# Dense products of a transformer layer written as four column tiles each, with the scheduler's table of draws removed

## The chip, the cores and the metric

The kernel runs on one core of a Trainium2 chip. The metric is the device time of one execution in microseconds (us). The kernel before took a median of 1049.04 us over three runs (1048.99 to 1049.08).

## What is computed

One macaron layer in fp32 on x of shape (4, 1024, 256): a feed-forward half step, causal attention with 16 heads of 16 features, a second feed-forward half step with the same weights.

```python
x = x + 0.5 * ffn(layernorm(x))
x = x + attn(layernorm(x), Wq, Wk, Wv, Wo)
x = x + 0.5 * ffn(layernorm(x))

def ffn(x):                      # 256 -> 704 -> 256
    g = (x @ gate_w.T) * gate_s
    u = (x @ up_w.T) * up_s
    return ((silu(g) * u) @ down_w.T) * down_s

def attn(x):                     # 16 heads of 16
    q, k, v = x @ Wq.T, x @ Wk.T, x @ Wv.T       # rotary embedding on q and k
    p = softmax(q @ k.T / 4 + causal_mask)
    return (p @ v) @ Wo.T
```

## The kernel before, in words

**Blocks.** The 4096 tokens are cut into 8 blocks of 512 (`BLK`); two blocks make one sequence of the batch. Each block goes through `ffn(i, 1)`, `qkv(i)`, the attention of four groups of four heads (`max_half`, `row_of_max`, `exp_half`, `weigh`, `attended`), `project` and `ffn(i, 2)`.

**Three shapes of product.** TensorE works in three shapes, and the planner names them `full`, `row` and `col`.

- `full`: the stationary operand is 128 rows by 128 columns. These are the dense products: gate and up (line 582, 512 wide), down (line 649, 256 wide), the features of q and k (line 723, 512 wide), the values (line 762, 256 wide) and the output projection (line 1104, 256 wide). The transposes at the start and in block 0 (lines 478 and 523) and the transpose that turns the row of maxima (line 943) have this shape too.
- `row`: a head has 16 features, and lies on 16 or 17 of 32 partitions. Four such products stand one above the other in the array. These are the scores for the maxima (line 863, q stationary) and the scores again for the exponentials (line 978, k stationary, one more row carries the negative maximum).
- `col`: the weighted values (line 1025). The stationary operand is 128 keys by 32 columns of one head, and four heads stand side by side, each with moving data of its own and each with 32 of the 128 output partitions.

An fp32 product is one instruction in the program, and the trace shows it as two loads of weights (LDWEIGHTS) and two passes (MATMUL). A transpose is one load and one pass.

**Order.** Every instruction is written out by a planner in Python (`Planner`, line 51). It keeps a clock for each engine with estimated durations, and at each step places the operation that can start first. Score halves are placed in pairs, called bursts: usually one half for maxima and one for exponentials. Up to `VISIT = 2` bursts follow one another before PE goes back to other work; below, such a stretch of one or two bursts is a visit. `GAP` is the least PE time between visits, `LONG` the PE time up to which a visit is put off until its second burst can follow, `WAIT` and `CHANGE` are what a change of shape is given, `HOLD` and `PATIENCE` delay a `col` product while PE is in shape `full`. `DRAWS` (line 23) is a table of 36 seeds, one for every 8 bursts (`draw`, line 155): a seed varies these constants and adds random numbers to the priorities.

**The row of maxima.** DVE writes each head's negative maxima to a column of `nm` (line 915, place by `row_at`, line 847). When a group is complete, PE transposes 128 columns of `nm` (line 943) so that the group's 16 columns land on 16 partitions of a bank, ACT copies them to `nmT` (line 948), and SP sends them by DMA to the free row of `qT` (line 953).

Of the kernel before, what the change touches and what calls it, by code (L numbers as in the profile page):

```python
# [19 lines left out]
P = 128  # L20
EPS = 1e-5
MASKED = -1e30
DRAWS = (
    490404, 660007, 210038, -148846, 520673, 329115, 0, 984430, -467682, -480220, 442636, -673967, -166110,
    -50883, 108124, 486735, -702287, -116672, -983856, -198212, 600534, -536043, -117586, -276618, -971831,
    -28682, -76214, -968411, -277199, -633759, -338722, 457662, -446958, -796892, -654951, -323475,
)


class Buf:  # L30
# [6 lines left out]
class Op:  # L37

    def __init__(self, eng, us, emit, deps=(), takes=(), uses=(), prio=5, tail=0.2, mode="full"):
        self.eng, self.us, self.emit, self.tail, self.mode = eng, us, emit, tail, mode
        self.takes, self.uses, self.prio = list(takes), list(uses), prio
        self.deps = [d for d in deps if d is not None]
        self.then = []
        self.done, self.waiters, self.pending, self.order = None, [], None, None
        for b in self.takes + self.uses:
            b.left += 1


class Planner:
# [1 line left out]


    ENGINES = ("pe", "dve", "act", "pool", "dma")
    GAP = 2.0
    LONG = 8.0
    VISIT = 2
    SECOND = 0.3
    OPEN = 3.0  # L60
    DUE = 0.5
    WAIT = dict(full=0.1, row=0.1, col=0.3)
    CHANGE = dict(full=0.2, row=0.2, col=0.12)
    HOLD = 0.8
    PATIENCE = 4.0

    STRETCH = 8

    def __init__(self, kinds, shared, draws=()):
        self.draws, self.bursts, self.luck, self.random = draws, 0, dict.fromkeys(self.ENGINES, 0.0), None  # L70
        self.draw()
        self.shared = shared
        self.busy = dict.fromkeys(self.ENGINES, 0.0)
        self.free = {k: [(0.0, i) for i in range(n)] for k, n in kinds.items()}
        self.loose = {e: [] for e in self.ENGINES}
        self.queues = {e: {} for e in self.ENGINES}
        self.mode, self.since, self.visit = "full", 9.0, 0
        self.alloc = None
        self.log = []
        self.added, self.unplaced = 0, 0  # L80
# [74 lines left out]
    def draw(self):  # L155

        if self.bursts % self.STRETCH:
            return
        n = self.bursts // self.STRETCH
        seed = self.draws[n] if n < len(self.draws) else 0  # L160
        for k in ("GAP", "LONG", "SECOND", "DUE", "HOLD", "PATIENCE", "OPEN"):
            setattr(self, k, getattr(Planner, k))
        self.luck = dict.fromkeys(self.ENGINES, 0.0)
        if seed:
            r = self.random = Random(abs(seed)).random
        if seed < 0:
            for k in ("GAP", "LONG", "SECOND", "DUE", "HOLD", "PATIENCE", "OPEN"):
                setattr(self, k, getattr(Planner, k) * (0.97 + 0.06 * r()))
        elif seed:
            self.GAP, self.LONG, self.SECOND = 0.8 + 1.8 * r(), 4.0 + 5.0 * r(), 0.05 + 0.5 * r()  # L170
            self.DUE, self.HOLD, self.PATIENCE, self.OPEN = r(), 1.6 * r(), 2.0 + 4.0 * r(), 1.0 + 3.0 * r()
            self.luck = {e: max(0.0, 4.0 * r() - 2.0) for e in self.ENGINES}

    def step(self, burst):
# [5 lines left out]
        for eng in self.ENGINES:  # L180
            for c in self.candidates(eng):
                s = max(c[0], self.busy["pe"] + 0.05) if eng == "pe" else c[0]
                if c[2].mode == "col" and self.mode == "full" and self.busy["pe"] < self.ready(c[2]) + self.PATIENCE:
                    s += self.HOLD
                if eng == "pe" and due and any(k.slot is None and k.kind == "d" for k in c[2].takes):
                    s += self.DUE
                key = (s, c[1] + (self.luck[eng] * self.random() if self.luck[eng] else 0.0))
                if best is None or key < best[0]:
                    best = (key, c)
# [59 lines left out]
def tile_macaron(  # L249
# [59 lines left out]
    for kind, (n, _) in shapes.items():  # L309
# [13 lines left out]
    lasting = dict(  # L323
        kT=[cpool.tile([P, NG, BLK], F32, name=f"kT_{i}", tag=f"kT_{i}") for i in range(3)],
        hL=[cpool.tile([P, BLK], F32, name=f"hL_{i}", tag=f"hL_{i}") for i in range(1)],
        nm=[cpool.tile([P, P + 32], F32, name=f"nm_{i}", tag=f"nm_{i}") for i in range(3)],
        va=[cpool.tile([P, NB, H * VS + HP - VS], F32, name=f"va_{i}", tag=f"va_{i}") for i in range(4)],
    )

# [90 lines left out]
    def norm(i, j, src, prio, kind):  # L420
# [51 lines left out]
        ]  # L472
        return a, [*b, *v, c, d, *e], list(zip(xns, e))

    def idle(d, n):

        for _ in range(n):
            nc.tensor.matmul(d.tile[:, :P], ident, ident, start=True, stop=True)
# [36 lines left out]
    def turned(pair, j, xnT, prio, later, view, idles=0):  # L515

        ds = [Buf("d") for _ in range(NC)]

        def emit():
            idle(ds[0], idles)  # L520
            for c, d in enumerate(ds):
                for n, (xn, _) in enumerate(pair):
                    nc.tensor.transpose(d.tile[:, ts(n, P)], xn.tile[:, ts(c, P)], ident)  # L523

        def copy(c):
            (nc.vector.tensor_copy if c else nc.scalar.copy)(
                view(xnT.tile[:, c])[:, j - 1 : j + 1],
                ds[c].tile[:, : 2 * P].rearrange("p (j a t) -> p j a t", j=2, t=HP),
            )

        t = Op("pe", 4 * 0.107, emit, [p[1] for p in pair], [*ds, xnT], [p[0] for p in pair], prio=prio)
        k = [Op("act", act_us(D), partial(copy, 0), [t], uses=[ds[0], xnT], prio=later)]
        return t, [*k, Op("dve", dve_us(D), partial(copy, 1), [t], uses=[ds[1], xnT], prio=later)]


    def ffn(i, which):
# [38 lines left out]
        def product(d, cols, takes, parts=1):  # L575

            n = NB // parts
            for part in range(parts):
                for k in range(NC):

                    def emit(k=k, j=part * n):
                        nc.tensor.matmul(  # L582
                            d.tile[:, j * P : (j + n) * P],
                            wgu_sb[:, k, cols],
                            view(xnT.tile[:, k])[:, j : j + n],
                            start=(k == 0),
                            stop=(k == NC - 1),
                        )

                    need = [*(copies[part * NC : part * NC + NC] if parts > 1 else copies), gu_loaded]  # L590
                    first = not part and not k
                    o = Op(
                        "pe", mm_us(BLK // parts), emit, need, takes if first else [], [xnT] if first else [d, xnT], prio=3
                    )
                    mids.append(o)
            return o
# [43 lines left out]
        for j in range(NB):  # L640

            def down(j=j):
# [3 lines left out]

                def emit(n):
                    c = chunks[n]
                    nc.tensor.matmul(  # L649
                        d.tile[:, :D], hT[c].tile[:, ts(j, P)], wd_sb[:, c, :], start=(n == 0), stop=(n == NI - 1)  # L650
                    )

# [43 lines left out]
    def qkv(blk):  # L696
# [21 lines left out]
        def features(g):  # L718
# [1 line left out]
            d, qc, qs = Buf("d"), Buf("qc"), Buf("qs")  # L720

            def product(k):
                nc.tensor.matmul(  # L723
                    d.tile, wqkv_sb[:, k, ts(g, P)], xnT.tile[:, k, :], start=(k == 0), stop=(k == NC - 1)
                )

# [31 lines left out]
        def values(j):  # L758
            d = Buf("d")

            def product(n, k):
                nc.tensor.matmul(  # L762
                    d.tile[:, ts(n, D)],
                    xnT.tile[:, k, ts(j + n, P)],
                    wqkv_sb[:, k, 2 * D :],
                    start=(k == 0),
                    stop=(k == NC - 1),
                )
# [77 lines left out]

    def row_at(g, part, h, j):


        return g % 2 * P + part * GH * NB + h * NB + j  # L850

    def max_half(blk, unit, pair, nm, reduces):

# [24 lines left out]
        def head(e):  # L878
# [14 lines left out]
            if unit[0][0] != unit[-1][0]:  # L893
                j, part = unit[0][1:3]

                def reduce():
                    o = row_at(0, part, 2 * pair + e, j)
                    nc.vector.tensor_reduce(
                        nm.tile[:, o : o + P + 1 : P],
                        sc[e].tile.rearrange("p (g k) -> p g k", g=2),  # L900
                        AX.X,
                        ALU.max,
# [25 lines left out]
    def row_of_max(blk, g, nm, reduces):  # L928
# [11 lines left out]
            loose_att.extend(need)  # L940

        def turn():
            nc.tensor.transpose(d.tile[:, :P], nm.tile[:, g % 2 * HP : g % 2 * HP + P], ident)  # L943

        def copy():

            r = g % 2 * (P - HP)
            nc.scalar.copy(t.tile, d.tile[r : r + GH * NB, :P])

        def send(pair):  # L950
            for h in (2 * pair, 2 * pair + 1):
# [3 lines left out]
                    in_=t.tile[a : a + NB, :],  # L955
                )

        p = Op("pe", 0.107, turn, need, [d, t], [nm], prio=1)
        c = Op("act", act_us(P), copy, [p], uses=[d, t], prio=1)
        loose_att.append(c)  # L960
        for pair in (1, 0):
# [137 lines left out]
    def project(blk, j, aTs):  # L1099
        e = Buf("d")  # L1100

        def product():
            for c in range(NC):
                nc.tensor.matmul(  # L1104
                    e.tile[:, :D], aTs[c].tile[:, ts(j, P)], wo_sb[:, c, :], start=(c == 0), stop=(c == NC - 1)
                )

# [203 lines left out]
```

## Time and profile before

| | |
|---|---|
| median of 3 runs | 1049.04 us |
| the profiled execution | 1049.1 us |
| its span, first to last instruction | 1047.4 us |
| TensorE: busy, passes | 1041.7 us (99%), 6550 |
| granted TensorE clock | 1.000 of full speed |
| VectorE (DVE), ScalarE (ACT), GpSimd (POOL) busy | 809.2, 431.4, 295.2 us |
| packets of PE's instruction queue | 51 of 16 KB |

Busy time of PE counts a pass from its start to its modelled end, and passes overlap: a pass of 512 columns is listed with some 600 ns, while the next one starts 429 ns after it. So the mean duration of a PE group says less than the distance between two starts, and the working below goes by starts.

### The profile page before, as it was taken

The numbers are of one execution on the slowest core, as the hardware profiler recorded it, in microseconds if no ns is written. First come the engines' busy times: TensorE is split into PE (matmuls) and PEld (weight loads), VectorE is DVE, ScalarE is ACT, GpSimd is POOL, SyncE is SP. The second block draws the span as 40 slices with busy tenths as digits, with TensorE's granted clock in tenths as the row PEclk, the third lists the DMA queues.
The fourth block names the chain that finished last, engine by engine and source line by source line (L and its number), as shares of the span: only waits on it lengthen the run. The fifth ranks groups of instructions, "written<-read, shape, count | busy, mean of one in ns | idle before, by whom it ended". The sixth has DMA issues, their size and how long they took to land.

```text
span 1047.4 us, 17496 instructions
## 1 busy us (share of the span) xinstructions
PE 1041.7 (99%) x6550; PEld 535.2 (51%) x6550; DVE 809.2 (77%) x1876; ACT 431.4 (41%) x821; POOL 295.2 (28%) x501
## 2 busy tenths in 40 slices
PE   9999999999999999999999999999999999999998
PEld 5655554454545644553544554543645544535365
DVE  6679879788898887778888797698898876884342
ACT  3215333344454353444434443355354443453511
POOL 5322521431131622412204524221216211121210
PEclk9999999999999999999999999999999999999999
DMA  8211202101010110111111012001021010010000
GB/s 289 60 41 42 48 15 61 41 22 41 21 42 22 41 42 21 37 46 37 38 29 31 12 42 41 31 13 41 2 62 42 11 51 2 21 42 11 11 21 20
DMA packets 37924, 40.38 MB, mean 39 GB/s; under 512 B 3984, under 2 KB 27728, under 8 KB 37712
## 3 DMA queue, kind: packets, MB, share of 16 engines
q1 hardware_dynamic: 37184, 38.81, 13.5%
q8 instruction: 51, 0.84, 0.3%
q10 hardware_dynamic: 656, 0.47, 0.2%
q14 instruction: 33, 0.27, 0.1%
HBM read 19.60 MB, written 15.20 MB: 33 GB/s over the span
## 4 chain that ended last, share of the span: by engine, by line
PE 98%; DVE 1%; DMA 0%; ACT 0%; issue 0%; SPq 0%; DVEq 0%
PE bank L582 29%; PE bank L863 17%; PE bank L649 17%; PE bank L1025 13%; PE bank L978 10%; PE bank L723 5%; PE bank L1104 3%; PE bank L762 3%; PE bank L943 0%; DMA x<-in_x 0%; PE bank L523 0%; DVE nm L915 0%; DVE bank L888 0%; ACT pT L987 0%; DVE st L425 0%
## 5 line engine op out<-in xcount | busy, mean ns | idle before, releaser
L987 ACT ACTIVATE pT<-bank 128x512 f32<-128x512 f32 x576 | 299.4, 601 | 316.3 <-PE bank L978 315.3
L915 DVE TENSOR_REDUCE nm<-bank 128x1 f32<-128x512 f32 (+2 forms) x640 | 331.0, 573 | 25.8 <-PE bank L978 25.3
L582 PE MATMUL bank<-xnT,wgu_sb 128*128 128x512 f32 (+1 forms) x708 | 320.9, 598 | 0.2 <-ACT pT L987 0.2
L863 PE MATMUL bank<-kT,qT 16*128 16x512 f32 (+3 forms) x1536 | 291.1, 509 | 0.5 <-DVE hT L629 0.5
L978 PE MATMUL bank<-qT,kT 17*128 17x512 f32 (+3 forms) x1536 | 291.4, 513 | 0.0
L999 POOL TENSOR_SCALAR_AFFINE_SELECT pT<-pT 128x256 f32<-128x256 f32 x256 | 99.4, 407 | 406.4 <-ACT pT L987 405.7
L582 PEld LDWEIGHTS bank<-xnT,wgu_sb 128*128 128x128 f32 x708 | 127.8, 190 | 163.3 <-issue 121.3
L863 PEld LDWEIGHTS bank<-kT,qT 16*128 16x128 f32 x1536 | 112.9, 184 | 134.1 <-issue 38.2
L649 PE MATMUL bank<-wd_sb,hT 128*128 128x256 f32 x640 | 150.0, 380 | 0.0
L1025 PE MATMUL bank<-pT,va 128*32 128x512 f32 (+3 forms) x1536 | 137.1, 490 | 0.0
L649 PEld LDWEIGHTS bank<-wd_sb,hT 128*128 128x128 f32 x640 | 121.0, 190 | 19.1 <-issue 2.9
L888 DVE TENSOR_TENSOR bank<-bank,causal 128x256 f32<-128x256 f32 (+1 forms) x320 | 103.8, 370 | 25.9 <-PE bank L978 22.1
L978 PEld LDWEIGHTS bank<-qT,kT 17*128 17x128 f32 x1536 | 111.7, 184 | 8.3 <-issue 4.0
L623 ACT ACTIVATE ta<-bank,gus_sb 128x512 f32<-128x512 f32 x80 | 55.0, 688 | 115.0 <-PE bank L582 110.3
L626 DVE SCALAR_TENSOR_TENSOR ta<-ta,bank 128x512 f32<-128x512 f32 x80 | 54.8, 685 | 51.5 <-ACT ta L623 50.6
L1025 PEld LDWEIGHTS bank<-pT,va 128*32 128x32 f32 x1536 | 44.1, 109 | 94.0 <-issue 65.4
L629 DVE SCALAR_TENSOR_TENSOR hT<-bank,gus_sb,ta 128x512 f32<-128x512 f32 x80 | 59.4, 743 | 17.6 <-PE bank L582 16.9
L655 DVE TENSOR_TENSOR x<-bank,x 128x256 f32<-128x256 f32 x64 | 26.7, 418 | 56.1 <-PE bank L649 56.0
L1064 POOL TENSOR_TENSOR oq<-oq 128x512 f32<-128x512 f32 x32 | 40.6, 1268 | 102.0 <-DVE oq L1061 95.6
L1061 DVE STREAM_TRANSPOSE oq<-bank 128x512 f32<-128x512 f32 x64 | 45.4, 709 | 22.3 <-PE bank L1025 22.0
L723 PE MATMUL bank<-xnT,wqkv_sb 128*128 128x512 f32 x128 | 60.2, 603 | 0.0
L734 POOL TENSOR_TENSOR qs<-qs,rope_sb 128x512 f32<-128x512 f32 x32 | 40.6, 1271 | 40.3 <-DVE qs L731 40.0
(61 smaller groups left out, 670.6 us busy)
## 6 DMA issues: line engine op xcount, KB each, us to landing
xd<-xs SPq DMA_DIRECT2D x84, 128.0 KB
xnT<-xd SPq DMA_DIRECT2D x21, 512.0 KB
kT<-qT SPq DMA_DIRECT2D x64, 64.0 KB
x<-in_x SPq DMA_DIRECT2D x7, 512.0 KB
out<-x SPq DMA_DIRECT2D x14, 256.0 KB
qT<-nmT SPq DMA_DIRECT2D x128, 2.0 KB
wgu_sb<-in_wgu SPq DMA_DIRECT2D x2, 512.0 KB
rope_sb<-in_rope SPq DMA_DIRECT2D x1, 1024.0 KB
```

The source lines that it names most:

```text
L582: nc.tensor.matmul(d.tile[:, j * P : (j + n) * P], wgu_sb[:, k, cols], view(xnT.tile[:, k])[:, j : j + n], start=(k == 0), stop=(k == NC - 1),
L623: nc.scalar.activation(a.tile, d.tile, AF.Tanh, scale=gus_sb[:, 0, c : c + 1])
L629: nc.vector.scalar_tensor_tensor(hT[c].tile, e.tile, gus_sb[:, 1, c : c + 1], a.tile, ALU.mult, ALU.mult)
L649: nc.tensor.matmul(d.tile[:, :D], hT[c].tile[:, ts(j, P)], wd_sb[:, c, :], start=(n == 0), stop=(n == NI - 1))
L723: nc.tensor.matmul(d.tile, wqkv_sb[:, k, ts(g, P)], xnT.tile[:, k, :], start=(k == 0), stop=(k == NC - 1))
L863: nc.tensor.matmul(sc[e].tile[:, c0 : c0 + w], qT[blk].tile[r, g, ts(j, P)], kt.tile[r, g, :w], start=True, stop=True,)
L888: nc.vector.tensor_tensor(d, d, causal.unsqueeze(1).to_broadcast([P, len(masked), P]), ALU.add)
L915: nc.vector.tensor_reduce(nm.tile[:, o : o + 1], sc[e].tile[:, c0 : c0 + w], AX.X, ALU.max, negate=True)
L978: nc.tensor.matmul(sc[e].tile[:, c0 : c0 + w], kt.tile[r, g, ts(k % NB, P)], qT[blk].tile[r, g, BLK - w :], start=True, stop=True,)
L987: nc.scalar.activation(pT.tile[:, e, :w], sc[e].tile[:, :w], AF.Exp)
L999: nc.gpsimd.affine_select(out=d, in_=d, compare_op=ALU.is_ge, fill=0.0, base=0, pattern=[[0, 2], [1, P]], channel_multiplier=-1,)
L1025: nc.tensor.matmul(av.tile[ts(r, HP), BLK - w :], va[base + k // NB].tile[:, k % NB, h * VS : h * VS + HP], pTs[u, r // 2].tile[:, r % 2, ...
```

## The change

Each dense product is written as four products with 32 stationary columns each, on four column tiles, with the same moving operand and 32 output partitions each. This is the shape of the weighted values, so only two shapes are left, `row` and `col`, but for the transposes of the start and of block 0. The row of maxima is turned by an ordinary product with the identity on one column tile (32 columns of `nm`), and `nm` shrinks from 160 to 64 columns. The table of draws is empty, `HOLD` and `PATIENCE` go, and `GAP`, `LONG` and one `WAIT` have other values.

```diff
-DRAWS = ( 490404, 660007, 210038, -148846, ... 36 seeds ... )
+DRAWS = ()
...
-    GAP = 2.0
-    LONG = 8.0
+    GAP = 0.8
+    LONG = 7.0
...
-    WAIT = dict(full=0.1, row=0.1, col=0.3)
+    WAIT = dict(full=0.1, row=0.1, col=0.1)
     CHANGE = dict(full=0.2, row=0.2, col=0.12)
-    HOLD = 0.8
-    PATIENCE = 4.0
...
-                if c[2].mode == "col" and self.mode == "full" and self.busy["pe"] < self.ready(c[2]) + self.PATIENCE:
-                    s += self.HOLD
...
-        nm=[cpool.tile([P, P + 32], F32, name=f"nm_{i}", tag=f"nm_{i}") for i in range(3)],
+        nm=[cpool.tile([P, 2 * HP], F32, name=f"nm_{i}", tag=f"nm_{i}") for i in range(3)],
...
+    def product_of(out, w, x, **kw):
+
+        for m in range(w.shape[1] // HP):
+            nc.tensor.matmul(out[ts(m, HP)], w[:, ts(m, HP)], x, **kw)
...
# gate and up; the same edit for down, q and k, values and the output projection
-                        nc.tensor.matmul(
+                        product_of(
                             d.tile[:, j * P : (j + n) * P],
                             wgu_sb[:, k, cols],
                             view(xnT.tile[:, k])[:, j : j + n],
...
-        return g % 2 * P + part * GH * NB + h * NB + j
+        return g % 2 * HP + part * GH * NB + h * NB + j
...
-            nc.tensor.transpose(d.tile[:, :P], nm.tile[:, g % 2 * HP : g % 2 * HP + P], ident)
+            nc.tensor.matmul(d.tile[:HP, :P], nm.tile[:, ts(g % 2, HP)], ident, start=True, stop=True)
...
-            r = g % 2 * (P - HP)
-            nc.scalar.copy(t.tile, d.tile[r : r + GH * NB, :P])
+            nc.scalar.copy(t.tile, d.tile[: GH * NB, :P])
```

Operations have the mode `col` unless they say otherwise; the transposes of `turned` say `full`. The planner begins in `col`.

## The prediction

> **What bounds the kernel.** I read the page's busy times first, then its chain, then the groups of PE by shape, then PE's waits, and last the timeline at two places.
>
> ```profile
> span 1047.4 us, 17496 instructions
> ...
> PE 1041.7 (99%) x6550; PEld 535.2 (51%) x6550; DVE 809.2 (77%) x1876; ACT 431.4 (41%) x821; POOL 295.2 (28%) x501
> ...
> PE 98%; DVE 1%; DMA 0%; ACT 0%; issue 0%; SPq 0%; DVEq 0%
> PE bank L582 29%; PE bank L863 17%; PE bank L649 17%; PE bank L1025 13%; PE bank L978 10%; PE bank L723 5%; PE bank L1104 3%; PE bank L762 3%; PE bank L943 0%; DMA x<-in_x 0%; PE bank L523 0%; DVE nm L915 0%; DVE bank L888 0%; ACT pT L987 0%; DVE st L425 0%
> ```
>
> TensorE is the bound: the chain is PE from end to end. The next view, waits that ended an idle time of PE, says that it hardly ever waits: 2.4 us in all, 1.7 of them before the first dense product.
>
> ```profile
> PE bank L478 <- POOL ident masks.py:199: 1.4, 1, 1.4
> PE bank L863 <- DVE hT L629: 0.5, 1, 0.5
> PE bank L523 <- ACT xn L451: 0.3, 1, 0.3
> PE bank L582 <- ACT pT L987: 0.2, 1, 0.2
> ```
>
> So the time is the sum of PE's passes and of what a change of shape costs, and both can be read from starts. First a dense stretch between two visits, then the weighted values between two visits (timeline of PE; columns: start us, us, line, operation, count).
>
> ```profile
> 96.67 1.98 PE L582 MATMUL bank<-xnT,wgu_sb 128*128 128x512 f32 x4
> 98.59 0.38 PE L863 MATMUL bank<-kT,qT 16*128 16x128 f32 x2
> ```
>
> ```profile
> 420.12 0.70 PE L863 MATMUL bank<-kT,qT 16*128 16x512 f32 x2
> ...
> 422.10 1.92 PE L1025 MATMUL bank<-pT,va 128*32 128x512 f32 x16
> 423.95 0.70 PE L863 MATMUL bank<-kT,qT 16*128 16x512 f32 x2
> ```
>
> Each stretch holds four steps of 512 columns: four passes of the full array there, four packs of four passes (16) here. In the trace's single starts both go 429 ns apart in the steady state; a 256 wide pass and a 256 wide pack both take 215.5 ns, a 128 wide one 109. **A pack of four column tiles costs what one full pass costs.** The rest is the change of shape: 98.59 - 96.67 = 1.92 us (1.914 in ns), less 4 x 0.429 = 1.716, leaves 0.198 for the full stretch; 423.95 - 422.10 = 1.85 (1.855) leaves 0.139 for the column stretch. Of the 0.198, 0.105 stand between the first two passes and 0.093 behind the last; of the 0.139, 0.025 and 0.113. Over the whole trace the excess of a column stretch is 0.138 to 0.146 us in all 64; of the 118 full stretches behind the first it has a median of 0.213 and a sum of 26.6 us. The visit ahead of the weighted values took 422.10 - 420.12 = 1.98, four packs of row tiles, 0.264 above 1.716.
>
> **The sum before.** Passes: 828 of 512 x 0.429 = 355.2; 1032 of 256 x 0.2155 = 222.4; 82 of 128 x 0.109 = 8.9; packs of the weighted values 123.8; packs of the scores 247.5. Together 957.8 us. Excess: 125 visits of two bursts at a mean of 0.308 and 38 of one at 0.225 = 47.1; full stretches 26.6; column stretches 64 x 0.142 = 9.1; the first transposes 3.4. Together 86.2. Sum 1044.0, and PE's last pass ends at 1044.08. Another 3.3 us to the span's end and 1.7 to the 1049.1 us of the profiled execution, which stands 0.06 above the median, are the same after.
>
> **The change, part by part.** The order of the changed program, engine by engine, has the same dense products, each as four of 32 columns.
>
> *Dense products on column tiles.* 1860 passes become 1860 packs (7440 passes). By the weighted values' row they last the same: 0. Bounds: nothing in the trace shows four tiles that read one and the same moving address, or the gate product's moving operand, which is read in runs of 32 columns. The nearest rows are the weighted values' packs (0 ns more) and, on the other side, the stagger inside such a pack: the fourth pass starts 45 ns behind the first (412.577, .608, .615, .622). If that showed in each dense pack it would be 1860 x 0.045 = 84 us. Nothing below zero, since 429 ns for 512 columns is also the steady distance of full passes, row packs and column packs alike. I take 0: in 64 stretches the stagger never showed, as each tile goes on to its next pass by itself.
> The Trainium skill speaks against this: "TensorE: Matmul & The Clock Gate", section "Measured speedup vs the span model", gives a pack the time of one matmul plus about 4 ns for each further tile. That would be 12 ns a pack, 1860 x 0.012 = 22 us (an estimate from that page) and would make the sum 1064; the 429, 215.5 and 109 ns between packs here say that it does not add up in a stream.
>
> *Issue.* PE's instructions rise from 13,100 to some 24,300, and a 256 wide pack needs eight in 215.5 ns, 27 ns each. Between two waits of PE's sequencer (379.975 and 380.128) lie 20 instructions, 7.7 ns each, and the densest 64 in a row took 0.985 us, 15.4 ns each. So the issue is fast enough: 0. Its fetches (16 KB, 256 instructions, 0.9 to 1.6 us in the trace, one in some 18 us) come at most every 6.9 us: hidden, if a fetch is asked for one packet ahead; if not, 44 more fetches x 1 us = 44 us.
> The same page's section "Wait — 56ns, not 53.3ns?" gives 62 ns for each matmul where microcode decodes; four a pack would make 248 ns of 215.5 and cost 1032 x 0.032 = 33 us (estimate). The 7.7 ns above speak against that state here.
>
> *Changes of shape.* Before: 346 changes; 163 visits, 118 full and 64 column stretches behind the first. After: 319 changes; 155 visits (133 of two bursts, 22 of one), 160 column stretches, 5 full ones (start and block 0). Visits: 133 x 0.308 + 22 x 0.225 = 45.9, that is 1.2 less. An excess of a visit depends on its form, not on its neighbours (512 wide forms: 0.279 to 0.291 whichever stands before or behind), so column stretches on both sides change nothing. Stretches: 160 x 0.142 = 22.7 and four full ones 0.8, together 23.5, against 26.6 + 9.1 = 35.7: **12.2 less**.
>
> *Turning the maxima.* The transpose is one pass, the product two: 32 passes of 0.109 more, +3.5. The profile shows the 32:
>
> ```profile
> L943 PE MATMUL bank<-ident,nm x32: 272/273/329, 77.8 to 950.6; 128*128 128x128 f32 x32
> ```
>
> ACT's copy (32) and SP's 128 DMAs to `qT` stay; DVE's reductions stay in number; POOL clears 64 instead of 160 columns, at the start and beside PE's first stretch. The copy of the maxima is later by 0.109 us; behind it wait a DMA and then the exponentials, for which PE has other work. These cost nothing while dense work is left beside them; without it, 32 x 0.109 = 3.5 again.
>
> *The table.* No instruction goes with it; the order changes. What waits for PE's order is each visit (banks that DVE's reductions, 681 ns for 512 columns, and ACT's exponentials, 601, have to leave first) and each weighting. DVE has 23% of its time free, ACT 59%, so only single places can be late. Before, the excess of all visits above the cheapest of their own form is 5.4 us: all that the drawn order lost by lateness there. An order without draws can lose between 0 (5.4 less) and, my estimate, three times that (10.7 more). The shortest stretch between visits is 1.7 us before and after, so the bursts are no denser. I take half as much again: +2.4.
>
> **Sum:** 1049.1 - 1.2 - 12.2 + 3.5 + 2.4 = **1041.6 us**, 0.7% faster.
>
> **Rivals.**
>
> *PE waits for the undrawn order.* The saving of 9.9 us (1.2 + 12.2 - 3.5) is used up when 155 visits are late by 64 ns each, or 21 of them by the 0.46 us of the largest wait seen between visits (L863 on L629). For it: the table is gone, and the least time between visits fell from 2.0 to 0.8 by the planner's clock. Against: 2.4 us of waits in 1047, a quarter of DVE free. At three times the lateness (+10.7) the time is 1049.9, no change; at 0.1 us a visit, 1049.1 - 9.9 + 15.5 = 1054.7.
>
> *The packs of dense products do not close up* (the slower side). Place: the steady distance of starts inside a dense stretch, best seen in the last 28 us, which are dense alone. Price: 1.86 us for each ns a pack. It decides from 4.0 ns on ((9.9 - 2.4) / 1860). At a quarter of the stagger, 11 ns, the kernel takes 1041.6 + 20.9 = 1062.5, at the full stagger 1126. For it: no row has four tiles on one moving operand. Against: the weighted values, 192 packs of 512 at 429 ns.
>
> *More than forecast.* The lateness falls rather than grows: 1039.2 without any addition, 1033.8 with none left.
>
> The change does what it says: the order shows every dense product with 32 output partitions.
>
> **Chances.** Forecast 0.73 (1037 to 1046.9); undrawn order eats the gain 0.12, of which 0.05 within 0.2% (1047 to 1051, about what a measurement here can tell from no change) and 0.07 slower; packs that do not close up 0.10, slower; more than forecast 0.05 (under 1037). So faster 0.78, same 0.05, slower 0.17. The range leaves out the 0.05 below, the packs' 0.10 and the far end of the undrawn order: 1037 to 1052.
>
> **What would show it.** Dense packs 429 and 215.5 ns apart; a dense stretch between visits of four 512 wide packs in 1.855 us; 155 visits with the same mean excess; 64 passes on the line of the turn; PE still over 98% of the chain; the waits of PE between visits at some 5 to 10 us; about 95 packets of instructions. Wrong it would be if dense packs stood further apart, if PEld or issue came into the chain, or if PE waited for DVE or ACT at many visits.

## The result and the profile after

The changed kernel takes 1046.26 us (median of 8 runs, 1045.38 to 1046.72) against 1049.09 us of the kernel before (8 runs): ratio 0.9972, 95% interval 0.9961 to 0.9983. It is faster by 2.8 us; forecast were 7.5 (1041.6). The profiled execution took 1046.28 us, its span 1044.4. A few executions of the runs below were granted less than the full TensorE clock: e8's profiled one and three of e3's six 0.998, e11's profiled one 0.63 (1772 us, so its trace is not used).

From the page of the changed kernel: busy times, the packets of PE's instruction queue (q8), and the chain by engine.

```profile
span 1044.4 us, 28697 instructions
...
PE 1036.3 (99%) x12162; PEld 442.7 (42%) x12162; DVE 808.5 (77%) x1876; ACT 429.7 (41%) x821; POOL 295.1 (28%) x501
...
q8 instruction: 95, 1.56, 0.6%
...
PE 92%; DVE 6%; DMA 1%; issue 0%; ACT 0%; SPq 0%; DVEq 0%
```

PE now runs 12,162 passes, as many as forecast, and 95 packets of instructions are fetched. But 6% of the chain has gone to DVE, where 1% was. The dense work itself does what was expected. A stretch of two products with the gate and up weights (four packs of 512 columns) between two visits, in PE's timeline (start us, us, line, operation, count):

```profile
196.62 0.59 PE L859 MATMUL bank<-kT,qT 16*128 16x512 f32 x2
196.64 0.59 PE L972 MATMUL bank<-qT,kT 17*128 17x512 f32 x2
197.16 1.92 PE L470 MATMUL bank<-xnT,wgu_sb 128*32 128x512 f32 x16
199.02 0.70 PE L859 MATMUL bank<-kT,qT 16*128 16x512 f32 x2
```

From 197.16 to 199.02 are 1.86 us (1.854 in ns): the 1.855 of the weighted values, 0.060 less than the same stretch in the full shape. The dense end of the kernel shows the 256 wide packs (same view):

```profile
1036.34 2.34 PE L470 MATMUL bank<-wd_sb,hT 128*32 128x256 f32 x40
1038.50 0.61 PE L470 MATMUL bank<-wd_sb,hL 128*32 128x256 f32 x8
1038.93 2.34 PE L470 MATMUL bank<-wd_sb,hT 128*32 128x256 f32 x40
```

From 1036.34 to 1038.93 lie the 12 packs of one output tile: 2.59 us, 0.216 each. Packs of four tiles that read one moving operand close up like those that read different ones. The turn of the maxima has its 64 passes:

```profile
L939 PE MATMUL bank<-ident,nm x64: 272/273/297, 81.5 to 946.7; 128*32 128x128 f32 x64
```

What is different from the forecast is the waiting. The view of PE's waits lists little more than before:

```profile
PE bank L475 <- POOL ident masks.py:199: 1.4, 1, 1.4
PE bank L859 <- DVE x L1104: 0.9, 1, 0.9
PE bank L520 <- ACT xn L443: 0.6, 1, 0.6
PE bank L859 <- DVE oq L1055: 0.5, 2, 0.3
PE bank L859 <- DVE hT L626: 0.4, 1, 0.4
PE bank L1019 <- DVE nm L911: 0.2, 1, 0.2
```

This view misses most of it: a 512 wide pass is listed with some 600 ns, so a next pass that starts up to 171 ns later than its 429 leaves no idle time in it. By starts it can be counted. I took the cheapest visit and the cheapest stretch of each form (the same products) over all traces of this study. What that takes above its passes is called the price of its change of shape below, and everything above the cheapest is called waiting (us, profiled executions, the first transposes and the last dense stretch left out):

| kernel | price of visits | price of stretches | waits | 
|---|---|---|---|
| before | 40.7 | 33.7 | 8.3 |
| changed | 39.7 | 22.6 | 14.1 |

Price: -12.1. Two passes for each turn: +3.5. Waits: +5.8. First transposes: +0.2. Sum -2.6, and PE's last pass ends 2.8 us earlier (1041.28 instead of 1044.08). The division into price and waits is an estimate: it depends on how forms are told apart. With forms told apart by their products and the number of each, the waits are 8.3 before and 13.5 after, and a form that occurs once in all traces (70 of 296) has none by construction.

The largest single wait between visits stands here (PE's timeline, then the chain over the same time):

```profile
166.33 3.66 PE L470 MATMUL bank<-wo_sb,aT 128*32 128x256 f32 x64
170.86 0.73 PE L859 MATMUL bank<-kT,qT 16*128 16x256 f32 x8 [0.86 <-DVE x L1104]
```

```profile
166.50 0.68 DVE bank L884 x2
167.17 1.31 DVE nm L911 x4
168.49 0.67 DVE bank L884 x2
169.16 1.31 DVE nm L911 x4
170.47 0.34 DVE x L1104
170.81 0.04 issue
170.86 1.16 PE bank L859 x15
```

The visit of 170.86 needs a bank that the output projection wrote. DVE's addition that empties it (L1104) runs only behind four masks (L884) and eight reductions (L911) of the visit before, and DVE works from 166.33 to 170.8 without a gap. A DVE that is busy 77% on the mean is full here.

### The profile page after: what moved, and what is told of

Same layout as the page of the kernel before. It is cut to its first block, busy times and chain, and to the rows that moved or that the text cites. A ratio compares the mean times of both kernels' runs of the same rounds, so it can differ in the third digit from the quotient of the medians.

```text
span 1044.4 us, 28697 instructions
## 1 busy us (share of the span) xinstructions
PE 1036.3 (99%) x12162; PEld 442.7 (42%) x12162; DVE 808.5 (77%) x1876; ACT 429.7 (41%) x821; POOL 295.1 (28%) x501
## 3 DMA queue, kind: packets, MB, share of 16 engines
q1 hardware_dynamic: 37184, 38.81, 14.1%
## 4 chain that ended last, share of the span: by engine, by line
PE 92%; DVE 6%; DMA 1%; issue 0%; ACT 0%; SPq 0%; DVEq 0%
PE bank L470 54%; PE bank L859 17%; PE bank L1019 12%; PE bank L972 10%; DVE nm L911 1%; DVE bank L884 1%; DVE xs L491 1%; DVE nm L894 1%; PE bank L939 0%; DVE hT L626 0%; DVE ta L623 0%; DMA xd<-xs 0%; PE bank L520 0%; DVE ta L603 0%; DVE hL L606 0%
## 5 line engine op out<-in xcount | busy, mean ns | idle before, releaser
L911 DVE TENSOR_REDUCE nm<-bank 128x1 f32<-128x512 f32 (+2 forms) x640 | 330.3, 573 | 20.0 <-PE bank L972 17.8
L470 PE MATMUL bank<-xnT,wgu_sb 128*32 128x512 f32 (+1 forms) x2832 | 321.5, 592 | 0.3
L859 PE MATMUL bank<-kT,qT 16*128 16x512 f32 (+3 forms) x1536 | 286.8, 511 | 2.2 <-DVE x L1104 0.9
L972 PE MATMUL bank<-qT,kT 17*128 17x512 f32 (+3 forms) x1536 | 286.7, 514 | 0.0
L470 PEld LDWEIGHTS bank<-xnT,wgu_sb 128*32 128x32 f32 x2832 | 92.0, 109 | 194.6 <-issue 122.1
L470 PE MATMUL bank<-wd_sb,hT 128*32 128x256 f32 x2560 | 152.4, 379 | 0.0
L884 DVE TENSOR_TENSOR bank<-bank,causal 128x256 f32<-128x256 f32 (+1 forms) x320 | 103.9, 370 | 20.3 <-PE bank L972 15.1
L972 PEld LDWEIGHTS bank<-qT,kT 17*128 17x128 f32 x1536 | 109.4, 184 | 9.4 <-issue 2.6
L470 PEld LDWEIGHTS bank<-wd_sb,hT 128*32 128x32 f32 x2560 | 85.4, 110 | 55.1 <-issue 2.6
L1019 PEld LDWEIGHTS bank<-pT,va 128*32 128x32 f32 x1536 | 51.7, 109 | 83.5 <-issue 59.9
L1058 POOL TENSOR_TENSOR oq<-oq 128x512 f32<-128x512 f32 x32 | 40.7, 1273 | 154.8 <-DVE oq L1055 151.9
L470 PE MATMUL bank<-xnT,wqkv_sb 128*32 128x512 f32 x512 | 60.6, 595 | 0.1
```

The costliest lines, as they stand in the source:

```text
L470: nc.tensor.matmul(out[ts(m, HP)], w[:, ts(m, HP)], x, **kw)
L859: nc.tensor.matmul(sc[e].tile[:, c0 : c0 + w], qT[blk].tile[r, g, ts(j, P)], kt.tile[r, g, :w], start=True, stop=True,)
L884: nc.vector.tensor_tensor(d, d, causal.unsqueeze(1).to_broadcast([P, len(masked), P]), ALU.add)
L911: nc.vector.tensor_reduce(nm.tile[:, o : o + 1], sc[e].tile[:, c0 : c0 + w], AX.X, ALU.max, negate=True)
L972: nc.tensor.matmul(sc[e].tile[:, c0 : c0 + w], kt.tile[r, g, ts(k % NB, P)], qT[blk].tile[r, g, BLK - w :], start=True, stop=True,)
L1019: nc.tensor.matmul(av.tile[ts(r, HP), BLK - w :], va[base + k // NB].tile[:, k % NB, h * VS : h * VS + HP], pTs[u, r // 2].tile[:, r % 2, ...
```

## The experiments

Two theories. **1:** the shape saves what was forecast, and the order without draws gave part of it back as waits. **2:** the waits come with the shape, since a PE that gets through its dense work faster runs into DVE whatever the order.

**e1, the shape alone, in the order of before.** The kernel before, with its table and constants; only the dense products and the turn are changed, so that the order of instructions stays on every engine.

```diff
 # before.py, the five dense products
-                        nc.tensor.matmul(
+                        product_of(
 # the turn
-            nc.tensor.transpose(d.tile[:, :P], nm.tile[:, g % 2 * HP : g % 2 * HP + P], ident)
+            nc.tensor.matmul(d.tile[:HP, :P], nm.tile[:, g % 2 * P : g % 2 * P + HP], ident, start=True, stop=True)
-            r = g % 2 * (P - HP)
-            nc.scalar.copy(t.tile, d.tile[r : r + GH * NB, :P])
+            nc.scalar.copy(t.tile, d.tile[: GH * NB, :P])
```

> The kernel before with its table, constants and order of instructions on every engine; only the dense products are written as four column tiles and the maxima are turned by a product on one. PE's order holds 163 visits, 168 column stretches and 5 full ones (335 changes). Theory 1 (the shape saves what was forecast, and the changed kernel lost part of it to waits of the order without draws): passes +3.5, stretches 168 x 0.142 + 0.8 = 24.7 instead of 35.7, so 1049.1 - 11.0 + 3.5 = 1041.6 us, with no more waits than before. Theory 2 (the waits come with the shape: a PE that gets through dense work faster runs into DVE and ACT whatever the order): 1045 to 1047, as the changed kernel.

Measured: 1045.88 us, ratio 0.9970 (0.9960 to 0.9981). Theory 2's number. By starts: price 64.6 instead of 74.4, waits 11.6 instead of 8.3, passes +3.5: -3.0, and -3.2 was measured. By this count the same order waits 3.3 us more with the new shape. The changed kernel is 0.4 us slower than e1, so most of what its forecast lacks is lacking here already, with the table and the order of before.

Before and e1 have the same visits in the same sequence, so that they can be compared one by one, without a price. PE's last pass ends 3.1 us earlier. The opening up to the first visit takes 1.0 us more, the 163 visits together 1.55 more, the stretches between them 5.9 less (9.4 less for changes of shape, 3.5 more for the second passes of the turns), the dense end 0.2 more. Of the 1.55 us, 1.49 lie in the 56 visits that follow a gate and up stretch, and 0.07 in the other 107. One of the 56, before and in e1:

```profile
309.12 0.70 PE L863 MATMUL bank<-kT,qT 16*128 16x512 f32 x2
309.23 0.75 DVE L629 SCALAR_TENSOR_TENSOR hT<-bank,gus_sb,ta 128x512 f32<-128x512 f32 x1 [0.26 <-PE bank L582]
310.04 0.19 PEld L863 LDWEIGHTS bank<-kT,qT 16*128 16x128 f32 x2 [0.60 <-DVE hT L629]
311.11 0.70 PE L582 MATMUL bank<-xnT,wgu_sb 128*128 128x512 f32 x1
```

```profile
309.09 0.70 PE L868 MATMUL bank<-kT,qT 16*128 16x512 f32 x2
309.25 0.75 DVE L634 SCALAR_TENSOR_TENSOR hT<-bank,gus_sb,ta 128x512 f32<-128x512 f32 x1 [0.36 <-PE bank L478]
310.05 0.19 PEld L868 LDWEIGHTS bank<-kT,qT 16*128 16x128 f32 x2 [0.65 <-DVE hT L634]
311.13 0.64 PE L478 MATMUL bank<-xnT,wgu_sb 128*32 128x512 f32 x4
```

The visit takes 1.99 us before and 2.04 in e1. DVE's product of gate and up (hT) reads the stretch ahead of the visit, and the second burst loads its weights right behind it. Before, hT starts most often 631 ns after the start of the stretch's last pass, in e1 661 or 681. In 31 of the 33 visits that grew by more than 10 ns, they grew by as much as the end of hT moved, within 5 ns. Other readers of dense products start later too: ACT's silu most often 660 instead of 630 ns after the last pass starts, DVE's addition behind the down product 446 instead of 416. The reader of the weighted values, which lie on column tiles in both kernels, has 660 in both. So the 30 to 50 ns come with the shape. This is read from traces of one order; no run changes this lag alone.

**e2, the table alone.** `DRAWS = ()` in the kernel before.

> The kernel before with an empty table and nothing else changed, so the planner finds another order (162 visits, 115 full stretches behind the first, 64 column stretches: 0.9 us less for changes of shape). Theory 1: PE waits more than before, by about as much as the changed kernel does, 4 to 5 us: 1052 to 1053. Theory 2: the table is worth nothing, 1048 to 1049.

Measured: 1054.49 us, ratio 1.0049 (1.0036 to 1.0063). The table is worth 5.4 us in the old shape, with the old constants. By starts the price falls by 0.8 and the waits rise from 8.3 to 14.4. This is near theory 1's number, 1.5 us above its range. So both are at work. From e2 to the changed kernel, both without a table, it is 8.2 us down: the shape with its constants. From before to e2 it is 5.4 up.

**e3, the old seeds in the changed kernel.**

> The changed kernel with the 36 seeds of the kernel before. The order is another one than in either (161 visits, 166 column stretches: 1.7 us more for changes of shape than the changed kernel). If the seeds are good only for the order they stood in (theory 1), PE waits as much as in the changed kernel or more: 1046 to 1050. If any drawn variation lowers the waits, 1043 to 1044.

Measured: 1052.5 us (1050.89 to 1054.5), ratio 1.0031 (1.0020 to 1.0043), later than expected and more scattered; the three of its six executions at the full clock took 1050.9 to 1051.6. Seeds that saved 5.4 us in one order cost 6.2 in another, 5 at the full clock.

**e4, the turn by the transpose.** As e1, with the transpose of before on line 943.

> As e1, but the 32 rows of maxima are turned by the transpose of the kernel before: one pass in the full shape, which now stands alone between column stretches. 32 passes of 0.109 less (3.5 us), 389 changes of shape instead of 335: 32 more full stretches at 0.2 and 22 more column stretches at 0.142 make 9.5. Theory of priced changes: 6 us above e1. If a short change into the transpose is free: 3.5 us below e1.

Measured: 1049.83 us, 4.0 above e1, where 6 were expected. By starts the price of the stretches is 8.2 above e1's (9.5 expected), the passes 3.5 below. A lone transpose between two shapes costs somewhat less than a whole stretch, but more than the second pass of the product: the product is right for this place.

**e5, e6, e7: DVE relieved.** The kernel before, the changed one and e1 without the additions of the causal mask ahead of the maxima. The maxima are then taken over masked keys too, so the softmax subtracts another number; the later mask on the exponentials stays.

```diff
                 def mask():
...
-                    nc.vector.tensor_tensor(d, d, causal.unsqueeze(1).to_broadcast([P, len(masked), P]), ALU.add)
+                    pass
```

> The kernel before without the 320 additions of the causal mask on DVE (103.8 us of its 809; the maxima are then taken over masked keys too, the later mask on the exponentials stays). PE's order is the same. Theory 1 (what PE loses beyond passes and changes of shape is waits on DVE, which the table holds small before): visits and full stretches lose at most 8 us to waits, so 1041 to 1046. Rival (waits on ACT or DMA): 1048 to 1049.

> The changed kernel without the same 320 additions, PE's order unchanged. Its visits stand 8.9 us above the cheapest of their forms and its column stretches 4 us above 0.142. Theory 1 (DVE): most of these 13 us go, 1033 to 1038. Rival (ACT or DMA, or the shape itself): 1045 to 1046.

> The kernel of e1 (column shape in the order of before) without the 320 additions. If the saving of the shape was lost to waits on DVE, it shows here against e5 in full: the difference of e7 to e5 should be near -7.5 us, as forecast for e1, where e1 stood 3.2 below before. If the shape itself saves less, the difference stays at 3 us.

Measured: e5 1047.42 us (ratio 0.9985, 0.9976 to 0.9993), e6 1041.34 (0.9926, 0.9913 to 0.9940), e7 1043.48 (0.9949, 0.9936 to 0.9961). The changed kernel gains 4.9 us, before 1.7: the masks' work on DVE cost the changed kernel 3.2 us more than the kernel before. At the place shown above the wait has gone (e6, PE's timeline):

```profile
166.07 3.66 PE L470 MATMUL bank<-wo_sb,aT 128*32 128x256 f32 x64
169.66 1.16 PE L859 MATMUL bank<-kT,qT 16*128 16x256 f32 x16
```

From the projection's start to the visit's 3.59 us instead of 4.53. In e6's chain DVE falls back:

```profile
PE 97%; DVE 2%; ACT 1%; DMA 0%; issue 0%; SPq 0%; DVEq 0%
```

But e6 expected 1033 to 1038 by theory 1: of 14.1 us of waits 9.5 stay. And e7 stands 3.9 below e5, not 7.5: the masks' work explains 0.7 us of what the shape lacks in the order of before. Compared one by one, e7's visits take 1.20 us more than e5's, 1.19 of it in the same 56 behind gate and up. The later start of their readers stays when DVE has less to do.

**e11, e12: DVE relieved further.** As e5 and e6, and the reductions read only the last 128 columns of each part, so that the maxima are those of a part of the keys.

```diff
-                            nm.tile[:, o : o + 1], sc[e].tile[:, c0 : c0 + w], AX.X, ALU.max, negate=True
+                            nm.tile[:, o : o + 1], sc[e].tile[:, c0 + w - P : c0 + w], AX.X, ALU.max, negate=True
...
-                        sc[e].tile.rearrange("p (g k) -> p g k", g=2),
+                        sc[e].tile.rearrange("p (g k) -> p g k", g=2)[:, :, P:],
```

> As e5, and the reductions of the maxima read only the last 128 of their 256 to 512 columns (680 ns become some 280), so that DVE works about 200 us less; the maxima are then those of a part of the keys. PE's order is unchanged. Theory 1 (PE's waits are on DVE): below e5 by 1 to 4 us, 1043 to 1046.5. Rival (what is left of the waits is ACT, DMA or a fixed price): 1047, as e5.

> The same on the changed kernel, PE's order unchanged. Theory 1: with next to no waits on DVE on either side the difference to e11 is that of passes and changes of shape alone, worked out from the cheapest visit and stretch of each form in the traces as -7 to -8.5 us, so 1035 to 1039. Rival (the shape itself saves only what the changed kernel shows): 3 us below e11.

Measured: e11 1047.48 us (ratio 0.9983, 0.9974 to 0.9992), e12 1042.05 (0.9928, 0.9914 to 0.9941). Neither is faster than with the masks alone left out. In e12 the 0.7 us above e6 lie in the opening: the first visit starts 0.8 us later, and the visits together take 0.15 us less than in e6. So what waits remain do not hang on how much these reductions give DVE to do. e12 stands 5.4 below e11; theory 1 had 7 to 8.5. This prediction failed.

**e8, a table for the new shapes.** 36 new seeds in the changed kernel, kept when the planner's own clock ended earlier, 4.6 us in all.

```diff
-DRAWS = ()
+DRAWS = ( ... 36 seeds ... )
```

> The changed kernel with a table of 36 seeds drawn for its own shapes: seeds were kept when the planner's own clock ended earlier, 4.6 us in all. The order has 158 visits (130 of two bursts, 28 of one) and 163 column stretches, which costs 0.3 us more for changes of shape (158 visits 46.3 instead of 45.9, 163 stretches 23.1 instead of 22.7, less rounding) than the changed kernel. Theory 1 (the forecast gain was there, and was lost to waits of an order without draws): the waits fall by 4 to 6 us as the table of before saves 5.4 in the old shape, 1040 to 1043. Theory 2 (the faster dense work meets waits on DVE in any order): 1045 to 1047.

Measured: 1045.23 us (1044.25 to 1047.35), ratio 0.9959 (0.9945 to 0.9972). 1.0 us below the changed kernel where 4 to 6 were expected. Its profiled execution, the slowest at 1047.35 us, shows 14.5 us of waits against 14.1, but some 2 us of these can be its lower clock (an estimate: 0.2% of 1045 us), so the trace does not tell whether the waits fell. 4.6 us on the planner's clock were not 4.6 us on the chip.

**e10, both.** e8 without the mask's additions.

> e8 without the 320 additions of the causal mask on DVE (the maxima are taken over masked keys too). If what e8 still loses is waits on DVE as in e6, 2 to 4 us below e8; if the drawn order already hides them as in before (e5: 1.7), 1 to 2 us below e8.

Measured: 1042.56 us, ratio 0.9937 (0.9925 to 0.9950), 2.7 below e8 and 1.2 above e6.

**e9, the old constants in the changed kernel.**

```diff
-    GAP = 0.8
-    LONG = 7.0
+    GAP = 2.0
+    LONG = 8.0
...
-    WAIT = dict(full=0.1, row=0.1, col=0.1)
+    WAIT = dict(full=0.1, row=0.1, col=0.3)
```

> The changed kernel with GAP 2.0, LONG 8.0 and WAIT col 0.3 as before, without a table. Its order has 195 visits (93 of two bursts, 102 of one) and 200 column stretches, 399 changes of shape instead of 319. If a change of shape costs what the trace of before says, wherever it stands: visits 93 x 0.308 + 102 x 0.225 = 51.6 instead of 45.9, stretches 40 x 0.142 more, 11.4 us in all, 1057 to 1059 and later still if PE also waits. If the constants cost only through waits: below 1050.

Measured: 1074.92 us, ratio 1.0245 (1.0231 to 1.0259), 28.7 above the changed kernel. By starts the price is 13.9 higher (48.0 and 28.2) and the waits 14.3 (28.4). The price was foreseen about right at 11.4, the waits only as a possibility. PE's waits of this kernel, the first lines:

```profile
PE bank L859 <- DVE ta L623: 7.7, 15, 0.8
PE bank L859 <- DVE hT L626: 1.9, 5, 0.5
```

The kernel that beats both is e6, 1041.34 us: the change with 320 DVE instructions fewer.

## Why the prediction was right and wrong

The direction was right, the size was not: 2.8 us instead of 7.5. The time of 1046.26 us lies at the upper edge of the range given for the forecast, 1037 to 1046.9.

- *PE is the bound, and its time is passes and changes of shape:* held for passes. The distance of dense packs is 429 and 215.5 ns like that of full passes, 109 between the passes of a turn. That it "hardly ever waits" did not hold: the waits view shows 0.7 us between visits before, and by starts there are 8.3.
- *A pack costs what a full pass costs; issue and fetches cost nothing:* right for PE's own stream. 95 packets came, as worked out. The two rules of the Trainium skill that spoke against it ("TensorE: Matmul & The Clock Gate", sections "Measured speedup vs the span model" and "Wait — 56ns, not 53.3ns?") would have shown as a distance over 429 or 215.5 ns, and did not. The prediction's densest 64 instructions in 0.985 us are not what the starts show: there they take 1.67 us, 26 ns each. Issue cost nothing all the same. What the term left out is the reader: a dense product is read 30 to 50 ns later than before.
- *Changes of shape, -13.4: this is the step that failed.* It took "column stretches on both sides change nothing" and gave the shape no waits of its own. e1 tests it alone. By the forecast's terms it should save 7.5 us, and it saved 3.2. These 4.3 us are nearly all of the 4.7 by which the forecast is off. The visits, put at no change, took 1.55 us more, nearly all behind gate and up products, where the reader's later start holds up the second burst. The first dense work and the stretches, put at 11.0 less, gave 8.4: the mean of 0.225 us for a full stretch held waits, and these stayed. The 78 full stretches between two visits that hold no turn fell from a median of 0.201 to 0.141, by 0.060 each, not by 0.083. Above these medians they hold 1.1 us before and 1.2 in e1. By the count of price and waits this is 1.2 us less price and 3.3 us of waits that the forecast put at nothing.
- *Turning the maxima, +3.5:* right, 64 passes.
- *The table, +2.4:* this was the forecast's only term for waits, and they rose by 5.8. From e1 to the changed kernel, where the order changes, they rose by 2.5 and the price fell by 2.3, so the term fits what it was meant for. That is in part luck. Half of 5.4 is 2.7, not 2.4; the table alone is worth 5.4 us in the old shape (e2), a new table 1.0 in the new one (e8), and the constants changed along with it (e9). No run parts table and constants in the step from e1. The bound given, 10.7, holds.
- *Together:* -9.9 + 2.4 was forecast. It came to -12.1 + 3.5 + 5.8 + 0.2 = -2.6; the price is 1.3 us off, the waits 3.4. Of the signs named, the packs, the stretch of 1.855 us, the 64 passes and the 95 packets came. The chain with 92% PE instead of 98, the 14 us of waits instead of 5 to 10 and the dearer visits did not fit. The rival of the undrawn order found part of the waits, the rival of packs that don't close up fell.
- *The sum before:* it leaves out the 1.44 us before PE's first pass and closes all the same. A recount gives 46.7, 25.7, 8.9 and 3.3 us of excess for visits, full and column stretches and the first transposes, 84.5 instead of 86.2.
- *Open:* with DVE relieved the changed kernel waits 9.5 us and before 6.7. Neither the amount of DVE's work (e11, e12) nor the drawn order (e10) explains the rest. In e6, with forms told apart as in the recount, 3.3 us of it stand in visits behind gate and up and 3.5 in visits behind the weighted values. For the first, e1 shows what the second burst stands behind; the second was not followed up. Why a product on column tiles is read later stays open too.

## What to carry to other kernels

When PE is full, count its time from start to start, and take the price of a change of shape from the cheapest stretch of its form, not from the mean: the mean holds waits, and here these did not leave with the change. A product has two ends, when PE goes on and when its reader can start, so look up both before its shape is changed: the 660 ns of the weighted values' reader, against 631 for gate and up, stand in the trace of before. A written-out order that was selected for one kernel is a part of that kernel: it was worth 5.4 us where it was found and cost 6.2 where it was not. If PE gets quicker beside an engine that is full at places, look at those places, not at its mean, and change nothing but the shape in one run, in the old order: that run told most here.

## What was not expected of the hardware

Packs of four column tiles on one moving operand stand no further apart than full passes even where the moving operand is read in runs of 32 columns, and a column stretch is cheaper to enter than a full one: 0.025 us between its first two passes instead of 0.105, for 0.113 instead of 0.093 at its end. PE took 24,300 instructions in 1042 us, 43 ns each and 27 ns in the dense end, without a gap in PE's waits that is put down to issue. And the reader of a product on column tiles starts 30 to 50 ns later than that of a full one (660 or 681 instead of 631 ns after the last 512 wide pass starts, 446 instead of 416 after a 256 wide one), though PE itself goes on at the same distance.
